# Crossbar transposes of 2048 columns issued as two of 1024 in an attention and feed-forward kernel

## The chip, the cores and the metric

One core of a Trainium2 chip runs the whole program. The metric is the device time of one execution in microseconds (us); before the change the median of three runs is 921.09 us (920.28 to 923.07). Another execution was profiled; views of that profile are shown below.

## What is computed

Two layers over two batches of 1024 tokens, 2048 wide, in float32 at the interface:

```python
# layer 1: x = x + fake_quant(layernorm(x)) @ fake_quant(ctx)
q1 = fake_quant(layernorm(x), x1_scale, x1_zp)
q2 = fake_quant(ctx_4096, x2_scale, x2_zp)
x = x + jnp.matmul(q1, q2)
# layer 2: x = x + ffn(layernorm(x))
base = y @ W_base.T + b_base                      # y = layernorm(x), 2048 -> 2048
h = jnp.einsum('td,erd->ter', y, lora_A)          # 8 experts of rank 16
lora = jnp.einsum('ter,eor,te->to', h, lora_B, w) * 2.0   # w: top 2 of softmax(y @ W_router.T)
x = x + base + lora
```

`fake_quant` rounds to 0..255 and scales back; the products are of small whole numbers, which 16-bit floats hold exactly. In layer 2 every operand is split into a high and a low float16 part, and three products of the parts are added.

## The kernel before

**Stages.** For each batch: load x and the context, normalize and quantize x (`ln1`), transpose it (tiles `qn` to `at`, 128 tokens by 2048 columns), multiply with the context (`gemm1` at L717 for batch 0; for batch 1 `gemm1w` at L831, a scheme with seven products in place of eight, which first forms sums of `at` halves, the tiles `as`, in `half_sums` at L781). Then the second normalization (`ln2`), and `y_prep` (L888), which makes for each pair p of 128-token blocks seven combinations of y (a11, a12, s1, a22, s2, s3, s4; the trace calls them `y_a` and `y_s`). Each goes through `emit` (L899): a float32 tile of 1024 columns is cast into the high half of a tile `nat`, the low half is the difference on VectorE (L905), and one transpose turns both halves together, 2048 columns, into `y`. `hmm` (L943) multiplies y with the LoRA and router weights, `router` (L976) makes the expert weights and transposes them (`hh` to `hT`), and `g2` (L1272) is the large product in four groups per half of the output columns, with the seven-product scheme again: for each of eight k steps a weight tile `w`, and for each pair p three products per operand (L1281). LoRA terms are added at L1297. `w_step` (L1069) loads and splits each `w` (loads `wt`, `wb`, `wc`, `ws`, `wn`; on VectorE L1091).

In batch 0 the first four blocks of x are transposed on TensorE instead (`turn`, L684). So there are 70 crossbar transposes: 12 of `at` (4 in batch 0), 56 of y (7 x 4 pairs x 2 batches) and 2 of `hT`. All are issued on SP's queue by `transpose` (L376), the same queue as every load and store.

**What sets the order.** Nothing is scheduled by hand: each step is a task with a duration, a due time (`prio`), and the buffers that it reads and writes, in parts where a buffer is declared with parts. `Plan.order` (L166) simulates the five engines with these durations and takes, for each free engine, the due task whose inputs and buffer slots are there; the program is emitted in the order of the planned starts, and each engine then runs its instructions in that order. Three things in it concern transposes: a transpose of `cols` columns is charged 1.35 + 0.22 x cols / 1024 us on SP (L377), and 0.82 us of DMA time per 1024 columns (`TURN_COST`); the plan lets an SP transpose end no earlier than 0.2 us before the landing of the DMA before it (L268-269); and at most 8 DMAs are under way (`LANES`, L246). All tiles of 4 KB per partition share 48 slots (`u`).

Of the kernel before, what the change touches and what calls it, by code (L numbers as in the profile page):

```python
# [12 lines left out]
F16 = mybir.dt.float16  # L13
# [4 lines left out]
ALU = mybir.AluOpType  # L18
# [3 lines left out]
P = 128  # L22
NB = 2
T = 1024
D = 2048
# [4 lines left out]
HK = KT // 2  # L30
NT = T // P
# [3 lines left out]
HD = D // 2  # L35
# [8 lines left out]
MM = 0.216  # L44
LANES = 8
# [37 lines left out]
LAND = 2.1  # L83
STORE_LAND = 1.15
TURN_LAND = 0.65
TURN_COST = 0.82
NEXT = {"DVE": 0.08, "ACT": 0.1}


# [19 lines left out]
class Plan:  # L109
# [56 lines left out]
    def order(self):  # L166
        self.rank()
        free = dict(SLOTS)
        busy = dict.fromkeys(("SP", "ACT", "DVE", "POOL", "PE"), 0.9)
        ready = {e: [] for e in busy}  # L170
        events = [0.0, 0.9]
        lanes = []
        dma_free = 1.2
        land = 0.0
        lag = 0.0
        for t in self.tasks:
            t.left = len(t.preds)
            if not t.left:
                for e in t.durs:
                    bisect.insort(ready[e], (t.prio, t.seq, t))  # L180
        held = set()
        first = set()
        queue = {}
        for t in self.tasks:
            t.need = {}
        for t in sorted(self.tasks, key=lambda t: (t.prio, t.seq)):
            for b in t.bufs:
                if b.tag in free and b not in first:
                    first.add(b)
                    t.need[b.tag] = t.need.get(b.tag, 0) + 1  # L190
            for tag in t.need:
                queue.setdefault(tag, []).append(t)
        for q in queue.values():
            q.sort(key=lambda t: (t.prio, t.seq))

        known = set()

        def wake(at):
            if at not in known:
                known.add(at)  # L200
                heapq.heappush(events, at)

        def fits(t):
            if any(b.tag in free and b not in held and t.need.get(b.tag, 0) == 0 for b in t.bufs):
                return False
            for tag, n in t.need.items():
                for u in queue[tag]:
                    if u is t:
                        break
                    n += u.need[tag]  # L210
                if free[tag] < n:
                    return False
            return True

        releases = []
        count = itertools.count()
        todo = len(self.tasks)
        now = -1.0
        while todo:
            if not events:  # L220
                raise RuntimeError("no progress")
            nxt = heapq.heappop(events)
            if nxt <= now:
                continue
            now = nxt
            while releases and releases[0][0] <= now:
                free[heapq.heappop(releases)[-1].tag] += 1
            for eng in busy:
                while busy[eng] <= now:
                    pick = None  # L230
                    q = ready[eng]
                    for n, item in enumerate(q):
                        t = item[2]
                        if t.ready > now:
                            continue
                        h = t.far if t.far is not None else HORIZON
                        if t.prio + lag > now + h:
                            wake(t.prio + lag - h)
                            if t.prio + lag > now + HORIZON:
                                break  # L240
                            continue
                        if t.dma is not None:
                            if dma_free > now + DEPTH:
                                wake(dma_free - DEPTH)
                                break
                            if len([x for x in lanes if x > now]) >= LANES:  # L246
                                break
                        if (eng == "DVE" and len(t.durs) > 1 and busy["ACT"] <= now
                                and t.prio > -100):
                            continue  # L250
                        if not fits(t):
                            continue
                        pick = t
                        break
                    if pick is None:
                        break
                    t = pick
                    t.eng, t.dur = eng, t.durs[eng]
                    for e in t.durs:
                        ready[e].remove((t.prio, t.seq, t))  # L260
                    for tag, n in t.need.items():
                        free[tag] -= n
                        queue[tag].remove(t)
                    held.update(t.bufs)
                    t.start = now
                    end = now + t.dur
                    if t.dma is not None:
                        if t.turn:  # L268
                            end = max(end, land - 0.2)
                        dma_free = max(end + 0.2, dma_free) + t.dma  # L270
                        t.done = dma_free + (
                            TURN_LAND if t.turn else STORE_LAND if t.store else LAND
                        )
                        land = max(land, t.done)
                        lanes = [x for x in lanes if x > now] + [t.done]
                    else:
                        t.done = end + 0.1
                        end -= NEXT.get(eng, 0.0)
                    busy[eng] = end
                    wake(end)  # L280
                    wake(t.done)
                    if t.pe is not None:
                        lag = now - t.pe
                    for b in t.bufs:
                        b.users -= 1
                        if b.tag in free:
                            b.last = max(getattr(b, "last", 0.0), t.done)
                            if not b.users:
                                heapq.heappush(releases, (b.last, next(count), b))
                                wake(b.last)  # L290
                    for s in t.succs:
                        s.left -= 1
                        s.ready = max(s.ready, t.done)
                        if not s.left:
                            for e in s.durs:
                                bisect.insort(ready[e], (s.prio, s.seq, s))
                            wake(s.ready)
                    todo -= 1
        return sorted(self.tasks, key=lambda t: (t.start, t.seq))
# [3 lines left out]
def xattn_ffn_kernel(ctx, tc, x, cx, scal, wT, bias, arT, bT, out):  # L303
    nc = tc.nc
# [5 lines left out]
    add = plan.add  # L310

    def buf(tag, shape, dt, name, parts=1):
        def make():
            return pool.tile(shape, dt, tag=tag, bufs=SLOTS[tag], name=name)

        return Buf(tag, make, parts, name)
# [57 lines left out]
            r=r, w=w, dma=nbytes * P / RATE, **kw)  # L374

    def transpose(dst, src, r, w, cols, **kw):  # L376
        add("SP", 1.35 + 0.22 * cols / 1024, lambda: nc.sync.dma_start_transpose(dst(), src()),  # L377
            r=r, w=w, dma=TURN_COST * cols / 1024, turn=True, **kw)

    def affine(dst, src, n, r, w, scale=None, bias=None, only=None, **kw):  # L380
# [247 lines left out]
    def ln1(S, b, i):  # L628
# [38 lines left out]
            if pe_turn:  # L667
                turn(aT, qn, h, n)
        if not pe_turn:
            transpose(aT.ap, qn.ap, [qn], [aT], D)  # L670
        S["at", i] = aT
        if first:
            warm = bank("warm")
# [214 lines left out]
    def y_prep(S, b, p):  # L888
# [8 lines left out]
            return t  # L897

        def emit(o, t):  # L899
            n = buf("u", [P, 2, HD], F16, f"nat_{o}_{b}_{p}")  # L900
            y = buf("u", [P, 2, HK, P], F16, f"y_{o}_{b}_{p}")
            S["y", p, o] = y
            affine(lambda: n.ap()[:, 0], t.ap, HD, [t], [n])
            add("DVE", 1.22,
                lambda: nc.vector.tensor_tensor(  # L905
                    n.ap()[:, 1], t.ap(), n.ap()[:, 0], ALU.subtract), r=[t], w=[n])
            transpose(
                lambda: y.ap().rearrange("p h k t -> p (h k) t"),
                lambda: n.ap().rearrange("p h c -> p (h c)"), [n], [y], D)

        def comb(dst, a, c, op):
            add("DVE", 1.22, lambda: nc.vector.tensor_tensor(dst.ap(), a.ap(), c.ap(), op),  # L912
# [63 lines left out]
    def router(S, b):  # L976
        hf = S["hf"]
        rt = buf("u", [P, NT * 76], F32, f"rt_{b}")
        hh = buf("u", [P, NT, 2, ER], F16, f"hh_{b}")
        hT = buf("u", [P, NT, 2, P], F16, f"hT_{b}")  # L980
        S["hT"] = hT

        def cut(o, *shape):
# [48 lines left out]
        def weigh():  # L1032
# [12 lines left out]
            lambda: nc.vector.tensor_tensor(  # L1045
                hh.ap()[:, :, 1], hf.ap()[:, :, :ER], hh.ap()[:, :, 0], ALU.subtract),
            r=[hf], w=[hh])
        transpose(
            lambda: hT.ap().rearrange("p t h c -> p (t h) c"),
            lambda: hh.ap().rearrange("p t h c -> p (t h c)"), [hh], [hT], D)  # L1050

    made = {}
    STORED = {
# [218 lines left out]
    def g2(S, b, f, cp, grp, k, p, t):  # L1272
# [17 lines left out]
        for bk, tt, j, fresh in LORA[f][grp]:  # L1290
# [9 lines left out]
                        skip_group_check=True,  # L1300
                    )

            add("PE", 3 * MM, lmm, r=[hT, lb], w=[ps], prio=t + 6 * MM)
        for bk, tt, c in EVAC[f][grp]:
            ps, xb = S[bk, p], S["c", cp, 2 * p + tt]

# [160 lines left out]
```

## Time and profile before

| | us |
|---|---|
| median of 3 runs | 921.09 (920.28 to 923.07) |
| the profiled execution | 919.79 |
| its span, first to last instruction | 918.0 |
| TensorE clock granted, mean | 0.994 of full |
| TensorE busy with matmuls | 897.9 |
| VectorE, ScalarE, GpSimd busy | 712.2, 401.5, 66.1 |
| DMA queue of SP | 242.33 MB, 87.0% of 16 engines' span |
| transposes: median from issue to landing | `y_s` 4.7, `y_a` 5.1, `at` 5.8, `hT` 6.0 |
| issue on SP of a transpose, shortest, median, longest: `y_s` | 1.394, 2.194, 7.442 |
| the same: `y_a` | 1.339, 2.950, 10.999 |
| the same: `at` | 1.730, 3.797, 7.952 |

How to read the views: in a list of waits a row names the engine and line that waited, who ended the wait, the sum in us, how often, and the longest. In a timeline a row has start, duration, engine (SPq is SP's own queue), line, operation, tiles as out<-in, and how many instructions are merged. In a table of windows a row has the stretch, its length, then for TensorE, its weight loads, VectorE, ScalarE and GpSimd the busy time and number of instructions, then the granted clock, the share of the DMA engines and their GB/s.

### The profile page before, as it was taken

How to read it: one execution, taken by the hardware profiler on the slowest of the kernel's cores; microseconds unless marked ns; L12 is line 12 of the kernel's file. 1: busy time of each engine (PE TensorE's matmuls, PEld its weight loads, DVE VectorE, ACT ScalarE, POOL GpSimd, SP SyncE). 2: the span in 40 equal slices, each digit the busy share in tenths (PEclk: the TensorE clock that was granted, in tenths of full speed). 3: DMA queues.
4: the chain of work that ended last, by engine and by line, in shares of the span. 5: the costliest groups of instructions: out<-in, count | busy, mean ns of one | idle time of the engine just before them, and what ended most of it. 6: DMA issues, size and time to landing. Idle time of an engine off the chain costs nothing. (4 is left out here: it accounts for less than half of the span.)

```text
span 918.0 us, 12390 instructions
## 1 busy us (share of the span) xinstructions
PE 897.9 (98%) x4514; PEld 430.2 (47%) x4514; DVE 712.2 (78%) x1267; ACT 401.5 (44%) x458; POOL 66.1 (7%) x256
## 2 busy tenths in 40 slices
PE   7999999999999999999998999999999999999998
PEld 5444445474444444444443444647444444444443
DVE  7999998989598975999978998999835353799131
ACT  5999676516064321423892575863200121234000
POOL 0024220000000000002621003000000000000000
PEclk8999999999999999999999999999999999999999
DMA  9999999998999999999999946999995169793021
GB/s 321 387 385 284 314 289 251 180 225 267 235 332 321 391 393 374 380 381 342 315 319 243 366 179 158 243 230 211 307 260 186 58 203 389 245 353 127 12 91 47
DMA packets 230733, 243.11 MB, mean 265 GB/s; under 512 B 152848, under 2 KB 165136, under 8 KB 230672
## 3 DMA queue, kind: packets, MB, share of 16 engines
q1 hardware_dynamic: 230672, 242.33, 87.0%
q8 instruction: 35, 0.57, 0.2%
q14 instruction: 26, 0.21, 0.1%
HBM read 163.65 MB, written 41.94 MB: 224 GB/s over the span
## 5 line engine op out<-in xcount | busy, mean ns | idle before, releaser
L1281 PEld LDWEIGHTS <-y_s 128*128 128x128 f16 x1536 | 150.1, 98 | 183.4 <-issue 2.8
L1281 PE MATMUL X<-w,y_s 128*128 128x512 f16 x768 | 207.2, 379 | 2.0 <-DVE w L1091 2.0
L1281 PE MATMUL Y<-w,y_s 128*128 128x512 f16 x768 | 207.0, 379 | 0.0
L1281 PE MATMUL X<-w,y_a 128*128 128x512 f16 x768 | 189.2, 379 | 0.0
L1281 PEld LDWEIGHTS <-y_a 128*128 128x128 f16 x1152 | 112.0, 98 | 133.0 <-DMA y_a<-nat_a 1.3
L723 PE MATMUL g<-b,at 128*128 128x512 f16 x512 | 114.6, 384 | 4.1 <-ACT b L387 2.0
L387 ACT ACTIVATE w<-wb,gW 128x1024 f16<-128x1024 f32 (+1 forms) x48 | 51.5, 1076 | 121.5 <-DVE wb L1152 56.6
L1281 PE MATMUL Y<-w,y_a 128*128 128x512 f16 x384 | 103.2, 379 | 0.3 <-DMA y_a<-nat_a 0.3
L723 PEld LDWEIGHTS <-at 128*128 128x128 f16 x512 | 50.1, 99 | 64.4 <-issue 4.4
L1309 DVE SCALAR_TENSOR_TENSOR xr<-X,uW,xr 128x512 f32<-128x512 f32 x64 | 46.5, 746 | 30.4 <-PE X L1297 24.0
L1309 DVE SCALAR_TENSOR_TENSOR xr<-Y,uW,xr 128x512 f32<-128x512 f32 x42 | 31.1, 745 | 46.7 <-PE Y L1297 30.9
L1091 DVE SCALAR_TENSOR_TENSOR w<-wb,gW,w 128x1024 f16<-128x1024 f32 (+1 forms) x48 | 56.9, 1193 | 8.1 <-ACT w L387 7.8
L435 POOL TENSOR_TENSOR sm<-sm 128x1 f32<-128x1 f32 (+1 forms) x48 | 14.2, 296 | 487.2 <-DVE sm L421 484.7
L771 ACT ACTIVATE sq<-x,sm 128x1024 uint8<-128x1024 f32 x32 | 36.4, 1139 | 25.7 <-DVE x L752 16.7
L387 ACT ACTIVATE b<-u,nz 128x1024 f16<-128x1024 uint8 x41 | 45.7, 1138 | 1.8 <-DVE bt L814 0.8
L387 ACT ACTIVATE u<-bs,sc,rec 128x1024 uint8<-128x1024 f32 x31 | 38.0, 1233 | 15.4 <-DMA bs<-in_cx_dram 14.5
L408 DVE BATCH_NORM_STATS2 sm<-x 128x6 f32<-128x512 f32 x64 | 40.9, 683 | 4.8 <-DMA x<-in_x_dram 4.8
L387 ACT ACTIVATE w<-wt,gW 128x1024 f16<-128x1024 f32 x14 | 16.1, 1148 | 64.7 <-DVE wt L1138 41.6
L387 ACT ACTIVATE q<-x,sm 128x1024 uint8<-128x1024 f32 x30 | 35.7, 1229 | 13.3 <-POOL sm L644 8.6
L387 ACT ACTIVATE nat_s<-yt_a 128x1024 f16<-128x1024 f32 x30 | 31.1, 1050 | 19.4 <-DVE yt_a L912 13.2
L843 PEld LDWEIGHTS <-at 128*128 128x128 f16 x256 | 24.9, 98 | 31.0 <-issue 1.2
L912 DVE TENSOR_TENSOR yt_a<-yt_a,yt_a 128x1024 f32<-128x1024 f32 x32 | 38.6, 1220 | 0.0
(188 smaller groups left out, 1158.7 us busy)
## 6 DMA issues: line engine op xcount, KB each, us to landing
bs<-in_cx_dram SPq DMA_DIRECT2D x64, 512.0 KB, 10.6
wt<-in_wT_dram SPq DMA_DIRECT2D x64, 512.0 KB, 7.6
wn<-in_wT_dram SPq DMA_DIRECT2D x32, 512.0 KB, 9.0
x<-in_x_dram SPq DMA_DIRECT2D x30, 512.0 KB, 7.7
spill<-x SPq DMA_DIRECT2D x28, 512.0 KB, 4.4
xr<-spill SPq DMA_DIRECT2D x28, 512.0 KB, 8.1
wb<-in_wT_dram SPq DMA_DIRECT2D x24, 512.0 KB, 8.0
out_dram<-xr SPq DMA_DIRECT2D x24, 512.0 KB, 6.1
```

Of the source, the lines that this page charges most:

```text
L387: nc.scalar.activation(o, i, AF.Copy if c is None else AF.Identity, scale=1.0 if a is None else a, bias=0.0 if c is None else c,)
L408: nc.vector.bn_stats(st[:, 2 * h + c], b.ap()[:, c * C : (c + 1) * C])
L435: e.tensor_tensor(t, r, r, ALU.mult)
L723: nc.tensor.matmul(ps.ap(), aT.ap()[:, k, :], S["b", c, k // 4].ap()[:, k % 4, :], start=k == 0, stop=k == KT - 1,)
L771: nc.scalar.activation(sq.ap(), xb.ap(), AF.Square, bias=a[:, 22 + j : 23 + j], accum_out=a[:, 24 + 2 * j + h : 25 + 2 * j + h],)
L843: nc.tensor.matmul(ps.ap(), a()[:, 4 * h + k, :], w.ap()[:, k, :], start=fresh and h + k == 0, stop=h == 1 and k == 3, skip_group_check=True,)
L912: add("DVE", 1.22, lambda: nc.vector.tensor_tensor(dst.ap(), a.ap(), c.ap(), op), r=[a, c], w=[dst])
L1091: lambda: nc.vector.scalar_tensor_tensor(w.ap()[:, 1, lo:up], src(), g, w.ap()[:, 0, lo:up], ALU.mult, ALU.subtract),
L1281: nc.tensor.matmul(ps.ap(), y.ap()[:, a, k, :], w.ap()[:, q, j * C : (j + 1) * C], start=k == 0 and fresh and i == 0, stop=k == HK - 1 and ...
L1309: nc.vector.scalar_tensor_tensor(xs, ps.ap(), uW[:, cp : cp + 1], xs, ALU.mult, ALU.add)
```

## The change

Every call of `transpose` that passed 2048 columns now passes 1024, twice. Buffers that were one piece for the planner get two parts, so that a half can go, and be read, by itself. In `emit` the first half (y's high part) is issued as soon as it is cast, ahead of the subtraction that makes the low part. `at` is turned in column halves, `hT` in halves of four token blocks. The planner's rule for transposes is replaced: 1.5 us on SP whatever the size, 1.0 us of DMA time per 1024 columns, and instead of the wait for the landing before it a ring of 5 places, of which a transpose takes 2 and any other DMA 1.

```diff
-TURN_COST = 0.82
+TURN_COST = 1.0
+TURN_ISSUE = 1.5
+RING = 5
+TURN_RING = 2
...
                         if t.turn:
-                            end = max(end, land - 0.2)
+                            room = RING - TURN_RING
+                            for at, n in sorted(lanes, reverse=True):
+                                room -= n
+                                if room < 0:
+                                    end = max(end, at)
+                                    break
...
-        add("SP", 1.35 + 0.22 * cols / 1024, lambda: nc.sync.dma_start_transpose(dst(), src()),
+        add("SP", TURN_ISSUE, lambda: nc.sync.dma_start_transpose(dst(), src()),
...
         if not pe_turn:
-            transpose(aT.ap, qn.ap, [qn], [aT], D)
+            for h in range(2):
+                transpose(
+                    lambda h=h: aT.ap()[:, h * HK : (h + 1) * HK, :],
+                    lambda h=h: qn.ap()[:, h * HD : (h + 1) * HD], [(qn, [h])], [(aT, [h])], HD)
...
-            n = buf("u", [P, 2, HD], F16, f"nat_{o}_{b}_{p}")
-            y = buf("u", [P, 2, HK, P], F16, f"y_{o}_{b}_{p}")
+            n = buf("u", [P, 2, HD], F16, f"nat_{o}_{b}_{p}", 2)
+            y = buf("u", [P, 2, HK, P], F16, f"y_{o}_{b}_{p}", 2)
             S["y", p, o] = y
-            affine(lambda: n.ap()[:, 0], t.ap, HD, [t], [n])
+
+            def turn_half(a):
+                transpose(lambda: y.ap()[:, a], lambda: n.ap()[:, a], [(n, [a])], [(y, [a])], HD)
+
+            affine(lambda: n.ap()[:, 0], t.ap, HD, [t], [(n, [0])])
+            turn_half(0)
             add("DVE", 1.22,
                 lambda: nc.vector.tensor_tensor(
-                    n.ap()[:, 1], t.ap(), n.ap()[:, 0], ALU.subtract), r=[t], w=[n])
-            transpose(
-                lambda: y.ap().rearrange("p h k t -> p (h k) t"),
-                lambda: n.ap().rearrange("p h c -> p (h c)"), [n], [y], D)
+                    n.ap()[:, 1], t.ap(), n.ap()[:, 0], ALU.subtract),
+                r=[t, (n, [0])], w=[(n, [1])])
+            turn_half(1)
...
-        transpose(
-            lambda: hT.ap().rearrange("p t h c -> p (t h) c"),
-            lambda: hh.ap().rearrange("p t h c -> p (t h c)"), [hh], [hT], D)
+        for q in range(2):
+            ts = slice(q * NT // 2, (q + 1) * NT // 2)
+            transpose(
+                lambda ts=ts: hT.ap()[:, ts].rearrange("p t h c -> p (t h) c"),
+                lambda ts=ts: hh.ap()[:, ts].rearrange("p t h c -> p (t h c)"),
+                [hh], [(hT, [q])], HD)
...
-            add("PE", 3 * MM, lmm, r=[hT, lb], w=[ps], prio=t + 6 * MM)
+            add("PE", 3 * MM, lmm, r=[(hT, [(2 * p + tt) // 4]), lb], w=[ps], prio=t + 6 * MM)
```

Since the order comes out of the plan, other tasks move too. In the changed program the queue of SP holds 140 transposes where it held 70. Most halves of a y tile stand directly behind each other; in the stretch that follows the first group of batch 1 and around `at_1_6` and `at_1_1` halves of different tiles alternate, and two stores of the output stand between the halves of those two. On ScalarE the cast `u_1_1_3_1` stands ahead of the quantization of x's block 7 where it stood behind it. The order on TensorE is the same but for small shifts, among them the readers of `hT` in batch 0, which come later; the order on GpSimd is unchanged.

More of the change, by code (lines that the diff above doesn't have):

```diff
@@ L173, in order @@
         dma_free = 1.2
-        land = 0.0
         lag = 0.0
@@ L245, in order @@
                                 break
-                            if len([x for x in lanes if x > now]) >= LANES:
+                            if len([x for x in lanes if x[0] > now]) >= LANES:
                                 break
@@ L273, in order @@
                         )
-                        land = max(land, t.done)
-                        lanes = [x for x in lanes if x > now] + [t.done]
+                        lanes = [x for x in lanes if x[0] > now]
+                        lanes.append((t.done, TURN_RING if t.turn else 1))
                     else:
@@ L979, in router @@
         hh = buf("u", [P, NT, 2, ER], F16, f"hh_{b}")
-        hT = buf("u", [P, NT, 2, P], F16, f"hT_{b}")
+        hT = buf("u", [P, NT, 2, P], F16, f"hT_{b}", 2)
         S["hT"] = hT
```

## The prediction

> **What bounds the kernel.** I read the page first, then who TensorE waited for, then the SP queue in order of time around those waits, then windows of a few microseconds for the DMA share. Page and waits of TensorE:
>
> ```profile
> PE 897.9 (98%) x4514; PEld 430.2 (47%) x4514; DVE 712.2 (78%) x1267; ACT 401.5 (44%) x458; POOL 66.1 (7%) x256
> ...
> PE X L1281 <- DVE w L1091: 2.0, 3, 0.9
> PE gY L843 <- DVE as L797: 1.7, 2, 1.4
> ...
> PE ph L953 <- DMA y_a<-nat_a: 1.5, 1, 1.5
> ...
> PE gX L843 <- DVE as L797: 1.6, 1, 1.6
> ...
> PE Y L1297 <- DMA hT<-hh: 0.3, 1, 0.3
> PE Y L1281 <- DMA y_a<-nat_a: 0.3, 1, 0.3
> ```
>
> TensorE is the bound: 918.0 - 897.9 leaves 20.1 us in which it stands. By the timeline about 6.7 of them lie in the first 24 us and 4.0 behind the last matmul; the change touches neither. What is left for it are the rows above: 2.0 (three stalls at 258 to 276), 3.3 (493 to 500), 1.5 (148.6), 0.3 (288) and 0.3 (607.8): 7.4 us, 0.8% of the time. More than that it cannot win. What it can lose is larger: 70 transposes stand on the one queue, SP, which also issues every load.
>
> How a whole transpose behaves there, in the SP queue's timeline, and the DMA in windows of the same place:
>
> ```profile
> 474.43 2.11 SPq L373 DMA_DIRECT2D bs<-in_cx_dram  x4
> 477.99 0.36 SPq L1224 DMA_DIRECT2D out_dram<-xr  x1
> 478.44 9.32 SPq L377 DMA_TRANSPOSE at<-qn  x2
> ```
> ```profile
> 478.44:483.30 4.86, 4.86 (x24) 2.23 (x23) 4.79 (x11) 4.60 (x5) 3.33 (x9) 1.00 1.01 357
> 483.30:484.40 1.10, 1.10 (x7) 0.49 (x5) 1.10 (x3) 0.00 (x0) 1.10 (x1) 1.00 2.60 214
> 484.40:485.60 1.20, 1.20 (x8) 0.55 (x6) 1.20 (x4) 0.00 (x0) 0.95 (x4) 1.00 0.18 22
> 485.60:487.20 1.60, 1.60 (x9) 0.72 (x8) 0.18 (x1) 0.53 (x1) 0.80 (x4) 1.00 1.09 245
> ```
>
> Behind five loads and stores the first of the two holds SP for 7.36 us (the last two numbers of a window are DMA share and GB/s). The loads drain until 483.3, a first part of the transpose goes, then for 1.2 us nearly nothing moves (share 0.18), then the rest. The store before it lands at 486.02 and the issue ends at 485.80: a whole transpose is let go only when the DMA before it has landed. The same holds between transposes. In a run of them each lands 2.4 to 2.6 us after the one before, and most issues end within 0.3 us of the landing before them:
>
> ```profile
> 169.71 1.75 SPq L377 DMA_TRANSPOSE y_s<-nat_s  x1
> ...
> 221.92 4.51 SPq L377 DMA_TRANSPOSE y_s<-nat_s  x2
> 226.53 0.82 SPq L373 DMA_DIRECT2D xr<-spill  x1
> 227.45 4.79 SPq L377 DMA_TRANSPOSE y_s<-nat_s  x1
> 232.34 0.53 SPq L373 DMA_DIRECT2D wc<-in_wT_dram  x1
> 232.96 13.21 SPq L377 DMA_TRANSPOSE y_s<-nat_s  x5
> ```
>
> 13.21 / 5 = 2.64 us each, at some 204 GB/s in this stretch.
>
> **The change, part by part.** *Removed*: 70 issues. *Added*: 140 of half the size, the same bytes and packets. TensorE, VectorE and ScalarE get the same work in nearly the same order.
>
> *The price of a half's issue* is in no row. Issues of wholes into an idle queue took 1.75 (169.7) to 2.18 us; the shortest of all 1.34 and 1.39. From below: at 169.7 the first packet left 1.18 us after the start; for a load it is 0.96 with an issue of 0.33, so 0.63 behind the issue; a transpose therefore begins to push after about 1.18 - 0.63 = 0.55 us, and half of what follows (1.34 - 0.55) gives 0.55 + 0.4 = 0.95. From above: nothing scales, 1.75. I take 1.34, the nearest row: a half should not need longer than the quickest whole. With 0.07 between issues a half costs 1.41, a pair 2.82. A gain stays possible: at 0.95 a pair is 2.04.
>
> A rule speaks against the change: the Trainium skill, page "DMA: Bandwidth & Descriptors", section "Rules for kernel authors", says to coalesce many small transfers into a large one. From that page's table (64 KB in 0.95 us, 1 MB in 6.15) I estimate a fixed part of 0.60 us per transfer, so +0.60 per pair: 2.64 + 0.60 = 3.24. The row speaks otherwise: here a whole pays no fixed part but the landing of its predecessor, and the empty 1.2 us above. I take the row's reading and keep 3.24 inside the range.
>
> *Three runs of transposes*, with SP's other issues in them taken as they are:
> - A, 169.7 to 199.2 (29.5 us): ten wholes. Twenty halves and 2.7 us of loads: 20 x 1.41 + 2.7 = 30.9. It was gated by the low half of a nat tile (VectorE, 1.22 us); the high half now goes without it, about one half earlier (1.4). End: 0.
> - B, 221.9 to 246.2 (24.3): eight. 16 x 1.41 + 1.35 = 23.9: -0.4. Its start hangs on a VectorE chain that makes the weights loaded behind A.
> - A', 608.8 to 641.9 (33.1): twelve. 24 x 1.41 + 1.3 = 35.1: +2.0. The last tile of A' lands 4.1 us before TensorE first reads it, and the first weight tile loaded behind has 3.2 us to spare: hidden. Without that cover it would cost the 2.0.
>
> *The stalls.* At 148.6 y_a of the second pair lands exactly when needed, at the end of an unbroken SP stretch from 120.0, which opens with a whole held for 11.0 us behind ten weight loads. A half can go when fewer loads are in flight, say two load times earlier for its first half (loads land about 1.4 apart there); the stretch then runs about 2 us ahead and the 1.5 us vanish. But TensorE comes that much earlier to 258, where w waits for loads issued behind run B (247.0 onward, DMA share about 1.0): what B does not give is waited there instead. Of 1.5 I count 0.7, of the 2.0 there B's 0.4, of the hT stall 0.3 (two halves, and TensorE's order moves its readers back). Batch 0: -1.4.
>
> At 493 the "as" sums stand on VectorE behind a cast of b that waited 3.29 us for ScalarE's u, which stood on ScalarE behind a q that waits for POOL. In the changed program's order that u comes before the q, and the four bs loads that feed it follow the first half of at_1_4 instead of the whole, which had held SP 7.84 us. The tile that the sums read (at_1_1, landed 490.3) is now the third of four halves. I count 2.5 of the 3.3, and 0.3 at 607.8. Batch 1: -2.8.
>
> *Moved waits.* Stores of out now stand between halves of at_1_6 and at_1_1 and wait for VectorE; the second halves queue behind them. at_1_6 was read 0.04 us after it landed, so its second half, now last of the four, may come late: +0.7. A half that waits for its nat tile on SP holds the weight loads behind it; that price is in the runs.
>
> Sum: -1.4 - 2.8 + 0.7 = -3.5. The profiled execution took 919.79 (span 918.0 and 1.8 around it), so 916.3; the median of the runs, 921.09, lies 1.3 above: 917.6.
>
> **Rivals.**
> 1. *A half's issue costs nearly a whole's* (slower). Each 0.1 us on a half adds 2.0 in A and 1.6 in B, both in front of the weights at 258, and 2.4 in A' less its 3.2 of cover. At 1.50 (1.57 with the gap): A 34.1 - 29.5 - 1.4 = +3.2, B 26.5 - 24.3 = +2.2, so batch 0 +5.4; A' 39.0 - 33.1 - 3.2 = +2.7 against the -2.5 at 493: about +5.6, 926.7. From the forecast's -3.5 at 1.34 and 3.6 per 0.1 it decides from about 1.44. For it: idle issues are 1.75 to 2.18 as a rule and 1.34 only twice, and the planner's own law for whole transposes (1.79, near those rows) charges 1.57 for 1024 columns. Against: the first-packet times, by which most of an issue is pushing.
> 2. *The holes go and halves are quick* (0.95 to 1.2): a pair takes at most 2.5. B ends 2 to 3 us earlier, the stalls at 258 vanish too: -1.5 - 2.0 - 0.3 - 3.3 - 0.3 = -7.4 at best, about -6: 915.
> 3. *Nothing to see*: the transposes' landings move, but the tight places are set by VectorE and ScalarE, and the 1.5 is waited again at 258. Then only 0.3 to 2 us go: 919 to 921.
>
> **Numbers.** Forecast (halves of 1.25 to 1.4, -2.8 to -4.5) 0.35; quick halves 0.13; nothing to see 0.26; dear halves 0.26. About 0.3% (2.8 us) is what a measurement of this kernel can tell from no change: faster below 918.3, slower above 923.9. Faster 0.48, within 0.27, slower 0.25. Range 914.2 to 925.5: best case nearly whole, dear halves up to about 1.5 with part of their loss hidden. The likeliest case alone: 916.5 to 918.3.
>
> **What would show it.** Right: 140 transposes whose median issue is below 1.45 us; no window of share under 0.3 inside a transpose that follows loads; the TensorE rows for y_a and "as" under 0.5 us in sum; B ends no later than 246. Wrong: issues of 1.5 us and more with the queue idle, B ending behind 248, and a grown row "PE X <- DVE w" in batch 0; or a new wait for at<-qn near 488.

## The result and the profile after

The changed kernel is slower: 934.61 us, median of five runs (930.72 to 935.40), against 921.09 us of the kernel before, run beside it on the same chip. The ratio is 1.0127, 95% interval 1.0105 to 1.0148: some 11.7 us lost by the ratio (13.5 between the medians), where a gain of 3.5 was forecast and the range ended at 925.5. The profiled execution took 930.72 us, 10.9 more than that of before.

TensorE has the same work (900.9 us busy, 3.0 more), but its idle time grew from 20.1 to 28.0 us. The list of who TensorE waited for, first rows:

```profile
PE X L1298 <- DVE w L1108: 4.9, 6, 1.4
PE ph L971 <- DMA y_a<-nat_a: 4.3, 2, 3.9
PE X L1298 <- ACT w L394: 2.2, 1, 2.2
PE wsum L600 <- DVE wacc L596: 2.2, 1, 2.2
...
PE gX L853 <- DVE as L807: 2.0, 2, 1.6
```

The waits for "as" did shrink (3.3 to 2.0), and of the one for y_a at 148.6 only 0.35 us are left (at 145.2). New ones stand in their place: for the first weight tile (ScalarE's and VectorE's half of `w`), for the sum of squares `wsum`, for y_a in batch 1.

The transposes' line, duration in ns as shortest/median/longest:

```profile
L384 SPq DMA_TRANSPOSE y_s<-nat_s x64: 1232/1292/6433, 128.6 to 689.6; - x64
L384 SPq DMA_TRANSPOSE y_a<-nat_a x48: 1231/1295/8019, 100.8 to 638.5; - x48
L384 SPq DMA_TRANSPOSE at<-qn x24: 1250/1737/4299, 69.3 to 504.2; - x24
```

So a half costs 1.29 us where the forecast took 1.34: the price was about right, and yet the result was not.

Windows around the two longest waits (the last three numbers are the granted clock, the DMA share and GB/s):

```profile
146.60:150.40 3.80, 0.47 (x3) 0.10 (x1) 3.71 (x9) 3.80 (x5) 0.00 (x0) 0.99 1.04 250
150.40:153.80 3.40, 3.07 (x8) 1.11 (x8) 3.40 (x5) 3.40 (x5) 0.00 (x0) 0.51 0.91 259
...
589.90:594.10 4.20, 0.29 (x4) 0.21 (x4) 3.48 (x12) 1.85 (x4) 0.00 (x0) 1.00 1.09 242
594.10:597.50 3.40, 3.40 (x23) 2.61 (x21) 0.70 (x4) 2.13 (x3) 0.00 (x0) 0.50 1.05 206
```

TensorE stands almost still for some 4 us, and then runs at half clock for 3.4 us, which costs another 1.7 us each time.

To see where time is lost, I matched TensorE's matmuls by the tiles they read and write, and took start time in one kernel minus start time in the profile of before (in us; the head of the table is the time in the profile of before; the column 560 is read at 565 to 570, where the orders run alike again):

| kernel | 140 | 160 | 280 | 340 | 480 | 560 | 600 | 900 |
|---|---|---|---|---|---|---|---|---|
| changed | -2.4 | 2.0 | 2.5 | 7.2 | 7.2 | 6.1 | 11.2 | 10.6 |
| e1, halves in the old order | -1.0 | 3.5 | 7.0 | 6.3 | 6.3 | 7.4 | 7.4 | 6.8 |
| e2, wholes in the new order | -1.4 | 2.2 | 2.2 | 4.8 | 4.8 | 5.0 | 10.3 | 9.7 |
| e10, new order with three places mended | -1.7 | -0.9 | 1.8 | 4.2 | 4.2 | 3.7 | 3.0 | 4.8 |
| e11, before once more | -1.2 | 4.2 | 2.0 | 4.0 | 4.0 | 5.1 | 5.1 | 4.8 |
| e12, e1 with one exchange | -0.4 | -0.6 | 2.6 | 3.0 | 3.0 | 2.2 | 2.2 | 1.6 |

In the changed kernel the loss comes in three steps: +4.4 at 150, +4.7 between 280 and 340, +5.1 around 590 (a gain of 1.1 lies between). The row e11 is a warning: the profile of before shown above was a quick execution of its kernel (919.79 us; its medians in the later sittings are 921.98 to 923.74), and a second one loses 4.8 us against it with not one instruction changed. So single steps of 2 to 5 us in one profile prove nothing; verdicts below are on the ratios.

### The profile page after: what moved, and what is told of

It is laid out like the page before. It is cut to its first block, busy times and chain, and to the rows that moved or that the text cites. A ratio compares the mean times of both kernels' runs of the same rounds, so it can differ in the third digit from the quotient of the medians.

```text
span 928.9 us, 12520 instructions
## 1 busy us (share of the span) xinstructions
PE 900.9 (97%) x4514; PEld 432.0 (47%) x4514; DVE 709.5 (76%) x1265; ACT 403.6 (43%) x460; POOL 64.5 (7%) x256
## 5 line engine op out<-in xcount | busy, mean ns | idle before, releaser
L1326 DVE SCALAR_TENSOR_TENSOR xr<-X,uW,xr 128x512 f32<-128x512 f32 x64 | 46.6, 746 | 43.1 <-PE X L1314 25.4
L394 ACT ACTIVATE u<-bs,sc,rec 128x1024 uint8<-128x1024 f32 x34 | 41.4, 1231 | 13.7 <-DMA bs<-in_cx_dram 13.3
L394 ACT ACTIVATE b<-u,nz 128x1024 f16<-128x1024 uint8 x38 | 42.6, 1139 | 9.2 <-DVE bt L824 7.5
L394 ACT ACTIVATE w<-wt,gW 128x1024 f16<-128x1024 f32 x16 | 18.0, 1145 | 65.0 <-DVE wt L1155 40.5
L394 ACT ACTIVATE yt_a<-x,sm 128x1024 f32<-128x1024 f32 x26 | 31.1, 1233 | 26.6 <-POOL sm L894 18.2
L394 ACT ACTIVATE q<-x,sm 128x1024 uint8<-128x1024 f32 x30 | 36.0, 1228 | 10.3 <-POOL sm L651 6.4
L971 PE MATMUL ph<-ar,y_a 128*128 128x136 f16 x192 | 36.1, 228 | 4.3 <-DMA y_a<-nat_a 4.3
L587 ACT ACTIVATE wn<-wn 128x1024 f32<-128x1024 f32 x20 | 21.0, 1052 | 41.8 <-DMA wn<-in_wT_dram 25.3
```

What stands on the lines that cost most here:

```text
L394: nc.scalar.activation(o, i, AF.Copy if c is None else AF.Identity, scale=1.0 if a is None else a, bias=0.0 if c is None else c,)
L587: nc.scalar.activation(d.ap(), s.ap(), AF.Square, accum_out=o)
L971: nc.tensor.matmul(ph.ap()[:, AR : 2 * AR], y[half].ap()[:, 1, k, :], ar[:, kr, :AR], start=False, stop=kk == KT - 1,)
L1326: nc.vector.scalar_tensor_tensor(xs, ps.ap(), uW[:, cp : cp + 1], xs, ALU.mult, ALU.add)
```

## The experiments

All ratios are to the kernel before on the same chip in the same sitting. Twelve more programs were run, e1 to e12; e11 is the kernel before once more.

| run | transposes | order on the engines | median us | ratio | 95% interval |
|---|---|---|---|---|---|
| changed | 140 halves | new | 934.61 | 1.0127 | 1.0105 to 1.0148 |
| e1 | 140 halves | old | 924.22 | 1.0004 | 0.9987 to 1.0022 |
| e2 | 70 wholes | new | 931.98 | 1.0109 | 1.0083 to 1.0135 |
| e3 | halves | new, idle time filled | 934.56 | 1.0127 | 1.0101 to 1.0153 |
| e4 | halves | third: halves, old rule | 933.20 | 1.0116 | 1.0096 to 1.0137 |
| e5 | wholes | fourth: wholes, new rule | 939.25 | 1.0173 | 1.0155 to 1.0191 |
| e6 | halves | new, VectorE's chain moved | 931.94 | 1.0103 | 1.0075 to 1.0132 |
| e7 | halves | new, ScalarE's square moved | 930.29 | 1.0077 | 1.0051 to 1.0104 |
| e8 | halves | new, SP's loads moved | 934.78 | 1.0125 | 1.0097 to 1.0152 |
| e9 | halves | new, e6 + e7 + e8 | 929.48 | 1.0073 | 1.0049 to 1.0098 |
| e10 | halves | new, e9 with e8 mended | 925.48 | 1.0039 | 1.0022 to 1.0055 |
| e11 | wholes | old (before once more) | 924.56 | one run | |
| e12 | halves | old, one exchange on ScalarE | 922.87 | 1.0009 | 0.9996 to 1.0022 |

### Price or order: e1 and e2

The change does two things at once: it issues halves, and it makes the planner order everything anew. e1 has the first without the second. The planner sees the steps and the rule of before; only what a step issues is doubled:

```diff
-        add("SP", 1.35 + 0.22 * cols / 1024, lambda: nc.sync.dma_start_transpose(dst(), src()),
+        def go():
+            d, s, h = dst(), src(), cols // 2
+            for q in range(2):
+                m = d.shape[1] // 2
+                nc.sync.dma_start_transpose(d[:, q * m : (q + 1) * m], s[:, q * h : (q + 1) * h])
+
+        add("SP", 1.35 + 0.22 * cols / 1024, go,
```

> The kernel before, with its plan and so its order on every engine untouched; only each of the 70 transpose steps issues two of 1024 columns in place of one of 2048. Theory A (the loss of 13.5 us comes from the new order that the plan makes of the changed steps and costs, not from what halves cost): a pair of halves measured 2.75 us against 2.64 for a whole in a run of them, so this is 917 to 922 us, ratio 0.996 to 1.001. Rival B (twice as many issues on SP are the loss): 929 to 936 us, ratio near 1.013, as with the whole change.

e2 has the second without the first: the changed plan, in which the first half's step issues nothing and the second's the whole.

```diff
-        add("SP", TURN_ISSUE, lambda: nc.sync.dma_start_transpose(dst(), src()),
+        add("SP", TURN_ISSUE, (lambda: nc.sync.dma_start_transpose(dst(), src())) if dst else
+            (lambda: None),
...
-                transpose(lambda: y.ap()[:, a], lambda: n.ap()[:, a], [(n, [a])], [(y, [a])], HD)
+                transpose(
+                    (lambda: y.ap().rearrange("p h k t -> p (h k) t")) if a else None,
+                    lambda: n.ap().rearrange("p h c -> p (h c)"), [(n, [a])], [(y, [a])], HD)
```

> The changed kernel's order on all engines, but 70 transposes of 2048 columns: the first half of each pair issues nothing, the second issues the whole. Theory A (order): still slow, 929 to 938 us, since TensorE, VectorE and ScalarE have the changed kernel's order; a little worse than the changed kernel is possible, since each first half is lost. Rival B (number of issues): back to 919 to 923 us.

Measured: halves in the old order 1.0004 (the interval is -1.2 to +2.0 us), wholes in the new order 1.0109. Theory A holds and rival B falls: the loss is in the order, and the 70 more issues cost nothing that can be measured in sum. In e1 the two halves of a tile stand directly behind each other and wait for the whole tile, so what a first half may gain by going early is not in it. The sum may hide a cost: run B of the transposes takes 26.9 and 25.9 us in the two kernels with halves in the old order (e1, and e12 below), against 24.3 and 23.5 in the two profiles of before, and TensorE then stands 3.0 and 3.1 us at 258 to 264 (1.2 and none in those two). A gain that would make up for it is not shown: the wait for y_a at 148, 1.5 and 3.5 us in the two profiles of before, is 0.9 in e12 but 2.8 in e1.

### The clock: e3

> The changed kernel with 30 matmuls of 240 columns (about 3 us, results overwritten or never read) put on TensorE ahead of the two waits after which its granted clock fell to half for 3.4 us: ahead of the first product of group 0 (148.9) and ahead of the second half of ph of block 2 in batch 1 (594). Theory C (the stall brings a second loss by the clock, about 1.7 us at each place): the clock stays full at both places and the time falls by about 3.4 us against the changed kernel, to about 931 us, ratio 1.009. Rival D (the low clock follows something else than TensorE's idle time, or the fill only takes the place of waiting): no change, 934 to 936, ratio 1.012 to 1.015.

```diff
+            if b == 1 and i == 2 and half:
+                fill(ph, 2 * AR, 240, 30)
...
+                if (b, f, grp, k, p, j) == (0, 0, 0, 0, 0, 0):
+                    fill(ps, 0, 240, 30)
```

`fill` issues matmuls of a constant tile, each opening a sum of its own in the bank named. In the bank of `ph` that also drops the first half of this block's sum, so this run leaves that half out of the block's LoRA and router values.

Measured: no gain (1.0127). At 150 the filling did what it was for: the clock stayed full, and TensorE was 2.3 us earlier at 160 than in the changed kernel. But by 340 the profile has nearly the lag of the changed kernel (6.7 and 7.2): what was won at one place was waited again at the next ones, and a low clock stands at 310 behind a wait that remains. At 594 the filling failed: y_a landed at 596.38 in this run, TensorE waited another 2.4 us behind the filling, and the clock fell at 597. So theory C was tested at one of its two places. There the low clock added to a wait, but the time at the end did not hang on it; of rival D its second part fits, that the filling only takes the place of waiting.

### Three places: e6, e7, e8, and together: e9, e10

Each moves steps in the plan's finished order:

```diff
-        return sorted(self.tasks, key=lambda t: (t.start, t.seq))
+        out = sorted(self.tasks, key=lambda t: (t.start, t.seq))
...
+        for keys, anchor in MOVES:
+            for key in keys:
+                t = find(key)
+                out.remove(t)
+                out.insert(out.index(find(anchor)) + 1, t)
+                anchor = key
+        return out
```

A line of `MOVES` holds the steps (engine, kind, buffer, which of them) and the step behind which they go.

**At 149** TensorE stands 3.7 us in two waits for the first weight tile. The scale gW of this tile hangs on `wsum`, which TensorE delivers at 141.94; in the new order VectorE has two normalization chains (some fifteen small steps on one number per token) ahead of the step that uses it, where the old order has one:

```profile
146.05 0.15 DVE L452 TENSOR_SCALAR wacc<-wsum 128x1 int32<-128x1 int32 x1
...
149.40 2.47 DVE L1108 SCALAR_TENSOR_TENSOR w<-wn,gW,w 128x1024 f16<-128x1024 f32 x2
```

The second row makes the low halves of the first two weight tiles. In the kernel before the same steps stand at

```profile
144.38 0.16 DVE L445 TENSOR_SCALAR wacc<-wsum 128x1 int32<-128x1 int32 x1
...
147.52 1.28 DVE L1091 SCALAR_TENSOR_TENSOR w<-wn,gW,w 128x1024 f16<-128x1024 f32 x1
```

There `wacc<-wsum` runs 0.04 us after its input, in the changed kernel 4.1 us after it. The second chain (2 us, of block 5, needed much later) is what e6 moves:

```diff
+    ([('DVE', 'newton', 'sm2_0_2', 1)], ('DVE', 'lo', 'w_0_0_0_0', 0)),
```

> The changed kernel with one step of VectorE moved: the small normalization chain of block 5 (2 us, in front of the weight scale gW in the changed order) goes behind the first weight tile, where the kernel before has it. Theory A1 (the loss sits in a few places where the new order puts a step before one that TensorE needs): gW is ready about 2 us earlier, the wait of 3.7 us at 149 falls to about 1.7 and the low clock there goes, so 2 to 3.5 us are won at 150; but as with the filled idle time they can be waited again at 260 to 322, where weight loads set the pace, so alone it gives 0 to -2 us: 932.5 to 935. Rival A2 (the loss is spread over many small shifts): nothing, 934 to 935.

**At 311** TensorE waits for `wsum` of the second half of the columns. The SP queue of the changed kernel shows why:

```profile
293.22 0.90 SPq L380 DMA_DIRECT2D wn<-in_wT_dram  x1
...
295.67 0.33 SPq L380 DMA_DIRECT2D wb<-in_wT_dram  x1
304.46 0.38 SPq L380 DMA_DIRECT2D wn<-in_wT_dram  x1
```

The last load of `wn` waits 8.5 us on SP, with all weight loads behind it. It is let go when ScalarE has squared the `wn` tile before it (304.44), a tile that itself landed 10 us after its issue. The built programs say what the load waits for: in the new order it was given the slot of that tile, in the old order the slot of a weight tile that TensorE had used up, and in the kernel before it goes 9 us earlier:

```profile
295.42 0.38 SPq L373 DMA_DIRECT2D wn<-in_wT_dram  x1
```

SP's order is the same in both here; what differs is when ScalarE's square stands in the order, and so whose slot comes free next. e7 puts the square behind one cast, where the old order has it:

```diff
+    ([('ACT', 'sq', 'wn_1_1', 0)], ('ACT', 'affine', 'w_0_0_3_2', 0)),
```

> The changed kernel with one step of ScalarE moved: the square of wn for k=1 (second half of the columns) goes behind one cast of a weight tile, as it stands in the kernel before. With that the last wn load is given the slot of a weight tile that TensorE has used up, as before, and no longer that of the wn tile ahead of it, for whose square SP was held 8.5 us at 296. Theory A1: the load is issued about 8 us earlier, the waits at 311 (wsum, 2.2) and 318 (w, 0.9) go and some of the one at 302: -3 to -4.5 us, 930 to 931.5, ratio 1.008 to 1.010. Rival A2: nothing, 934 to 935.

**At 594** TensorE waits for y_a of pair 1 in batch 1. SP's timeline in the changed kernel:

```profile
574.73 2.51 SPq L380 DMA_DIRECT2D wc<-in_wT_dram  x3
577.34 9.40 SPq L384 DMA_TRANSPOSE y_a<-nat_a  x3
...
587.97 8.73 SPq L384 DMA_TRANSPOSE y_a<-nat_a  x5
```

and in the kernel before:

```profile
578.61 7.45 SPq L377 DMA_TRANSPOSE y_a<-nat_a  x3
586.11 5.68 SPq L373 DMA_DIRECT2D wc<-in_wT_dram  x6
```

The new order sends weight loads ahead of the transposes that TensorE needs first: the half needed at 590 is issued at 587.97 and lands at 593.83. e8 moves three of these loads, and ScalarE's casts of them:

```diff
+    ([('SP', 'load', 'wc_1_1_0_2', 0), ('SP', 'load', 'wc_1_1_0_3', 0), ('SP', 'load', 'wc_1_1_0_4', 0)], ('SP', 'transpose', 'y_a12_1_2', 1)),
+    ([('ACT', 'affine', 'w_1_1_0_2', 0), ('ACT', 'affine', 'w_1_1_0_3', 0), ('ACT', 'affine', 'w_1_1_0_4', 0)], ('ACT', 'hmm', 'ph_1_2', 0)),
```

> The changed kernel with the three loads wc 2, 3 and 4 of batch 1's group 0 moved on SP behind the last y_a transpose of pair 2, and ScalarE's casts of them likewise, which is where the kernel before has them. Theory A1: y_a of pair 1 lands about 4 us earlier, the wait of 3.9 us at 590 to 594 goes to under 1 and the low clock behind it goes: -4 to -5.5 us, 929 to 930.5, ratio 1.007 to 1.009. Rival A2: the loads are then late themselves and the time is waited at w: 933 to 936.

> The changed kernel, all its halves, with the three moves together (VectorE's chain, ScalarE's square, SP's three loads). Theory A1: the gains add, -8 to -11 us: 924 to 927, ratio 1.001 to 1.004, so seven moved steps of some 3090 carry most of the loss. Rival A2: 931 to 935.

Measured. e7 came out as theory A1 said: its ratio is 0.0050 below the changed kernel's, about 4.6 us, and no wait for `wsum` is left. Its load goes at 297.98:

```profile
297.98 0.38 SPq L398 DMA_DIRECT2D wn<-in_wT_dram  x1
```

It is the only single move whose interval lies below that of the changed kernel, and that only just (1.0104 and 1.0105). e6 did at its place what was said: gW's step runs at 143.86, the idle time before the first products is 1.6 us and the clock stays full; but 2.3 us are waited at 259, where the changed kernel waited 0.6 (at 260.19), and its gain of 0.0024 lies within the intervals. e8 gave nothing, as A2 had it, though for a reason that neither theory had. The wait at 594 went (the lag at 600 is 4.8) and came back at 609 as a wait for w of 3.9 us with a low clock. The cause was my edit, in ScalarE's timeline of e8:

```profile
595.83 1.15 ACT L413 ACTIVATE w<-wc,gW 128x1024 f16<-128x1024 f32 x1 [5.00 <-DMA wc<-in_wT_dram]
```

The casts that I moved now stand ahead of casts of `yt` whose inputs were there, and hold ScalarE 5 us for a load; VectorE then stands from 599 to 605, and its half of w is late. e9, between the two theories with 1.0073, shows the same at its end (2.8 us of lag at 600, 9.4 behind it); it moves eight steps, not seven. e10 mends it: the casts go behind those of `yt`, and VectorE's low half of the first of these weight tiles goes behind a cast of `nat`.

```diff
-    ([('ACT', 'affine', 'w_1_1_0_2', 0), ('ACT', 'affine', 'w_1_1_0_3', 0), ('ACT', 'affine', 'w_1_1_0_4', 0)], ('ACT', 'hmm', 'ph_1_2', 0)),
+    ([('ACT', 'affine', 'w_1_1_0_2', 0), ('ACT', 'affine', 'w_1_1_0_3', 0), ('ACT', 'affine', 'w_1_1_0_4', 0)], ('ACT', 'affine', 'yt_a22_1_1', 0)),
+    ([('DVE', 'lo', 'w_1_1_0_2', 0)], ('DVE', 'affine', 'nat_a12_1_3', 0)),
```

> As with the three moves together, but the three casts of wc 2, 3 and 4 on ScalarE now go behind the casts of yt, which wait for no load; in the run before they stood ahead of them and held ScalarE 5 us at 591, and the 3.9 us came back at w 15 us later. Theory A1: the lag against the kernel before stays at about 3 us behind 600 (it grew from 2.8 to 9.4 there), so the profiled execution takes 921 to 925 us and the ratio is 1.000 to 1.004. Rival A2 (loads and transposes together are simply too much for the queue between 565 and 610, and any order waits): 928 to 931, ratio near 1.007.

Measured 925.48 us, ratio 1.0039 (1.0022 to 1.0055): the upper end of what A1 said. The intervals of e10 and of the changed kernel are far apart: nine moved steps give back 0.0088 of 0.0127, about 8 of 11.7 us, with all 140 halves in place. Rival A2 (the loss is spread, or the queue between 565 and 610 can't carry it in any order) falls for this part. How the 8 us divide among the three places is measured for e7 alone; the mended e8 was not run by itself. The remaining 0.4% was not taken apart.

### Rule or any new order: e4 and e5; before once more: e11

e4 keeps the halves as steps but gives the planner its old rule; e5 keeps wholes under the new rule. Their diffs are the lines of the change's diff that concern the rule (in e4 left out, in e5 alone put in).

> The changed kernel, halves as steps of their own that go and are read by themselves, but the planner's rule of before: 1.57 us for 1024 columns, 0.82 us of DMA time, and the wait for the landing before. Theory L (the new rule, which charges no wait for the landing before and lets the plan put loads ahead of transposes, made the bad order): near before, 919 to 926, ratio 0.998 to 1.004. Theory M (any change of the steps gives another order, and another order of a plan with so little slack costs some us in places that the plan doesn't see): slower than before again, 925 to 936, at other places.

> The kernel before, 70 transposes of 2048 columns in one piece, with the changed planner's rule: 1.5 us on SP, 2.0 us of DMA time for a whole, ring of 5 places. Theory L (the rule made the bad order): 928 to 936, ratio near 1.01. Theory M (any new order costs some us): somewhere in 922 to 934, at other places than in the changed kernel. If the halves as steps of their own are what made the order bad: 919 to 924.

> The kernel before once more, to see by a second profile how its stalls and its clock vary by themselves: 919 to 926 us, the waits for as at 493 to 500 there again (3.3), a low clock of 3.4 us behind one or two of the longest waits possible, none of the waits at 311 and 594.

Measured: 1.0116 and 1.0173. e4 is where theory M had it and theory L had not: without the new rule the order is bad too. e5, with 939.25 us, is slower than both theories said; by itself the new rule is enough for a bad order. So either half of the change to the plan makes an order that is 1% or more slower, at partly other places: e4 waits 3.9 us for "as" at 504 and 5.7 us in sum for w at 261 to 267, e5 4.6 us behind `hf` at 217 and 3.8 us at 510. The new rule does worst with wholes, so it does not need the halves to be bad. That leaves the old order as the special one; why it is better was not looked into. e11's expectation that its waits for "as" would be there again held (3.8 us); it also had the y_a wait at 149.9, 3.5 us and not 1.5, with 6.8 us at half clock behind it, and a wait of 1.4 us for w at 309.6, so a part of the wait near 311 comes without any change of order.

### The prediction's largest gain by itself: e12

```diff
+    ([('ACT', 'affine', 'u_1_1_3_1', 0)], ('ACT', 'affine', 'b_1_1_1', -1)),
```

> The kernel with halves in the old order, and one pair of steps of ScalarE exchanged: the cast of u (bs_1_1_3_1) goes ahead of the quantization of block 7 of x, as it stands in the changed order. This is the prediction's largest gain by itself: there it was to give 2.5 of the 3.3 us of the waits for as at 493 to 500. If that holds: these waits fall from 2.7 us (4.0 with the low clock) in the run with halves in the old order to under 1, and the time by about 2.5 us, to 921 to 922, ratio 0.997 to 0.999. If the next input is late too (at_1_1, which landed 490.3 in the kernel before): 0 to -1.5 us, ratio 0.999 to 1.001.

Measured 1.0009 (0.9996 to 1.0022): no gain to be seen, and no version of all these beats the kernel before. The waits for "as" are 2.2 us in sum and not under 1. TensorE's timeline of the kernel before, then of e12:

```profile
492.95 1.04 PE L843 MATMUL gY<-b,as 128*128 128x512 f16 x4 [1.42 <-DVE as L797]
...
496.48 1.04 PE L843 MATMUL gX<-bt,as 128*128 128x512 f16 x4 [1.63 <-DVE as L797]
```

```profile
494.47 1.04 PE L867 MATMUL gY<-b,as 128*128 128x512 f16 x4 [0.20 <-DVE as L821]
...
498.00 1.04 PE L867 MATMUL gX<-bt,as 128*128 128x512 f16 x4 [1.63 <-DVE as L821]
```

The first wait fell from 1.42 to 0.20. The second did not move at all: 1.63 before, 1.63 here. (In e1 the first was 2.45 and the second 0.16, since TensorE ran at half clock between the two and came later.) Between the first and the second "as" VectorE's order has three steps of 1.22, 0.75 and 1.22 us, whatever ScalarE does.

## Why the prediction was wrong

- **The bound, and the price of a half**: right. TensorE was and is the bound. A half costs 1.29 us against the 1.34 taken; in the last stretch of run B ten halves took 14.49 us, 2.90 per pair against 2.64 for a whole and 2.82 forecast, and below the 3.24 estimated from the table of the Trainium skill's page "DMA: Bandwidth & Descriptors", section "Bandwidth", which was measured on loads from HBM issued by GpSimd. (The 204 GB/s given beside the 2.64 are those of the whole of run B; the stretch of 13.21 us moved 228, with a load in it.) As a whole run B was mis-sized: 25.4 us where 23.9 was forecast, since three of its 16 halves were held for 2.1 us, two of them the second behind a load. The sum charged no half for waiting, but behind a load a second half waits for the landing as a whole did (last section). Run A ended 1.5 us earlier than before. Rival 1, dear halves, was not the cause of the loss: e1 bounds their price, net of what they gain, at 2.0 us.
- **The step that failed** is the sentence that TensorE, VectorE and ScalarE get the same work "in nearly the same order", which put the new order at nothing. The new order alone, with whole transposes (e2), costs 1.09%; the halves alone, in the old order (e1), 0.04%, which can't be told from nothing. The sum took every duration and every neighbour from the profile of before, and let a removed stall be filled by what came behind it. But the order is the plan's, and small shifts in it are what the stalls are made of: a 2 us chain ahead of gW, a square one place earlier, three loads ahead of three transposes. None was in the sum, neither as a cost nor in the range, whose slow end was made of SP's price alone.
- **148.6, "of 1.5 I count 0.7"**: the wait for y_a did go, but for 0.35 us, and TensorE came 3.7 us before w. What was late next was w: in the profile of before its low half was ready at 148.8, about when TensorE would have come without the stall, and in the new order about 2 us later. The sum had looked for the next wait at 258 and not at the next tile.
- **493 to 500, "2.5 of the 3.3"**: mis-sized. It is 1.3 in the changed kernel (3.3 to 2.0), and e12 shows the part of ScalarE's u to be 1.2 of it. I had put both waits down to the cast of b; the second belongs to VectorE's own order.
- **The moved wait at at_1_6, +0.7**: not there with halves; no row of TensorE names at<-qn. With wholes in the same order (e2) there is one, of 3.0 us at 495.7.
- **"More than that it cannot win"**: the 7.4 us left out two waits of before, 1.1 us for sm_bmax at 102.4 and 0.5 for x at 571.3. Neither is in the changed kernel's rows.
- **The hT stall**: gone from TensorE's rows, as forecast, worth 0.3.
- **A' hidden behind its cover**: held; no wait between 610 and 652 in the changed kernel, though its transposes ended at 652.5 (641.9 before).
- **What would make it wrong**: grown waits for w in batch 0 were named, and came (2.0 to 7.1 us over both rows), but as a sign of dear halves; issues of 1.5 us did not come, and B ended at 247.9, between the 246 of "right" and the 248 of "wrong". Of the signs of being right only the median issue came: the rows for y_a and "as" are 6.3 us in sum and not under 0.5, and stretches in which nearly nothing moves remain (share 0.07 from 667 to 668).

The changed order on each engine could be read before the run, and three places of it were (SP around at_1_6, u on ScalarE, hT on TensorE). The rest was called small shifts. By these runs a new order that this planner makes costs 1.2 to 1.7% in three of three cases, and of the changed kernel's 1.3% nine steps carry 0.9.

## What to carry to other kernels

Where a planner decides the order, an edit to one step's size or cost is an edit to the whole program: run the edit under the old order, and the new order without the edit, before putting a price on either. In reading two orders against each other, go to each place with little slack and ask of every in-order queue what now stands ahead of the step that is needed next, a slot's next owner included. And a wait that is taken away counts only up to the next input that is late.

## What the runs showed of the hardware

TensorE's granted clock falls to half after idle time, for 3.41 us or twice that. In each of the fourteen profiles all its changes lie whole multiples of 3.413 us apart, on a fixed grid. I cut the profiles, from 26 us on, into the stretches of that grid and summed TensorE's idle time in each (the ends of matmuls are modelled, so the limits are rough). Of the stretches at full clock, all 22 with 1.95 us or more of idle time were followed by one at half clock, 2 of 8 with 1.83 to 1.94, and none of some 3,600 with less. Of the stretches at half clock, all 8 with 0.62 us or more of idle time were followed by another, and all 24 with 0.58 or less by one at full clock. So what counts is the idle time inside one stretch: a stall of 2.33 us at 257.3 in e6, across two of them, left the clock full; one of 2.32 us at 146.2 in e1, nearly all in one, halved it for 6.83 us. Half the speed for 3.41 or 6.83 us is 1.7 or 3.4 us on top of the stall, and part of why one program differs by some us from run to run. The Trainium skill, page "TensorE: Matmul & The Clock Gate", Part 1, names such a free-running window, of 3413 ns. As the condition for the low clock it names one idle window; here about 2 us of idle time in a window sufficed.

A second half waits for landings as a whole does. In the changed kernel's SP queue, and its DMA in a window of the same place (share and GB/s last):

```profile
660.09 0.32 SPq L380 DMA_DIRECT2D xr<-spill  x1
660.51 7.72 SPq L384 DMA_TRANSPOSE y_s<-nat_s  x2
```
```profile
667.00:668.00 1.00, 1.00 (x6) 0.42 (x5) 0.00 (x0) 0.00 (x0) 0.00 (x0) 1.00 0.07 26
```

The first half's issue took 1.24 us; the second was held for 6.43, until 668.23, and the load ahead of the pair landed at 668.36. In the changed kernel 18 pairs of halves stand directly behind a load or store that landed more than 1.9 us after the first half's issue ended; in each of them the second half's issue ended between 0.42 us before that landing and 0.17 behind it. So a pair behind loads holds SP about as long as a whole transpose did (7.72 us here; the longest whole of y_s before took 7.44), and the stretch in which nearly nothing moves is there too.
